# Products of attention weights and values of two units in one PSUM bank of their own, behind each other

## The chip, the cores and the metric

The kernel runs on one core of one Trainium2 chip. The metric is the device time in microseconds (us) of one execution. The engines go by the names of the profile: PE is TensorE's matrix multiply, PEld its weight load, DVE is VectorE, ACT is ScalarE, POOL is GpSimd, SP is the engine that issues nearly all DMAs. Each engine runs its own instructions in the order in which they were issued to it; a wait at the head of an engine's queue holds up all that stands behind it.

## The reference

One decoder layer on 16 sequences of 128 tokens with width 256, all in float32. Three parts follow each other, each with a residual and a layer norm:

```python
# 1: causal attention, 16 heads of 16, only the 32 largest scores of a row are kept
scores = q @ k.T / sqrt(16)            # causal mask: -inf
vals, idx = top_k(scores, 32)
attn = softmax(scores kept at idx, -inf elsewhere)
x = layernorm(x + (attn @ v) @ Wo.T + bo)
# 2: 8 experts of 256 -> 512 -> 256, each token weighs every expert by its gate
o = einsum('eid,bsed->bsei', proj_out, relu(einsum('edi,bsi->bsed', proj_in, x)))
x = layernorm(x + sum_e o[..., e, :] * gate[..., e])   # gate: sums of ctx where itok == e
# 3: Hadamard transform, 4-bit rounding per token, ternary weights
x = layernorm(x + quantized(x @ H) @ ternary(weight).T)
```

## The kernel before

**Tiles and units.** The 16 sequences are cut into nine tiles t = 0 to 8 of 1, 1, 2, 2, 2, 2, 2, 2, 2 sequences (`SIZES`, L35). The attention of a tile is cut into units (t, c, b): c is one of two halves of the heads (8 heads, `HC`), b the sequence within the tile, and b runs fastest (L752). Tiles 0 and 1 have two units each (0, 1 and 2, 3); each later tile has four: units 4 to 7 are tile 2, units 20 to 23 tile 6, units 28 to 31 tile 8. The first two units of such a tile are its first half of heads (c = 0), the other two its second (c = 1).

**One unit.** `attn_scores` (L337) multiplies queries and keys into two PSUM banks, ACT copies them to `sc` (L346), POOL adds the causal mask (L352). `attn_weights` finds the 32 largest on DVE by four rounds of MAX8 (L381) and MATCH_REPLACE8 (L396), with a small scaling (L383) after the first; ACT takes exponentials (L372, L389). `attn_finish` sums them (L408), puts weights in place of the marks (L412, DVE) and divides by the sums (L416, POOL); the result is `wk`. `attn_turn` transposes `wk` on PE into two PSUM tiles, `pta` (L427, four transposes) and `ptb` (L428, one), and ACT copies them to `pT` (L437, five copies), of which there are two buffers that the units use in turn. `attn_apply` (L439) multiplies `pT` with the values `vm`: eight calls of a 32-column matmul (L445), each stored as two records in the trace, into the second quarter of the bank of `ptb`, and ACT copies the product with the bias to `oT` (L448, 128x128).

**The end of a tile.** `attn_end` multiplies `oT` by the output weights (`py`, L457), DVE adds the residual (L460) and begins a layer norm, for which ACT gives the inverse root (`rstd_a`, L230 and L232) and DVE does the rest (L239, L240, L259). PE transposes the result (L472), and the tile joins the queue of the experts.

**The experts** (`experts`, L507) are the bulk: up products (L554) into `ph`, ACT's relu (L558), down products (L521) into `po`, ACT's scaling by the gate into `part` (L529), and POOL's sum into `acc` (L532). Between them run the gates of a tile (L500 on DVE, pairs of them for two sequences), and, for the tile before, `ffn`: layer norm, Hadamard steps on POOL (L638), the rounding (L641 to L651, DVE), and the last product (L663, L618).

**What sets the order.** Nothing is planned by costs of an engine: the instructions are issued in the order of the Python program. A generator runs the attention in 9 steps a unit (`STEPS`, L789); a dictionary `plan` holds what else is done in a step (`at`, L797); and the loop at L898 puts expert work behind each step, so much that it keeps pace with the steps. The turn of a unit is 3 steps after its end (1 step for the last unit of a tile), its products are two steps behind its turn (L832):

Of the kernel before, what the change touches and what calls it, by code (L numbers as in the profile page):

```python
# [13 lines left out]
AF = mybir.ActivationFunctionType  # L14
# [3 lines left out]
P = 128  # L18
# [11 lines left out]
def decoder_kernel(ctx: ExitStack, tc: tile.TileContext, i: dict, out: bass.AP):  # L30
    nc = tc.nc
    NB, S, D = 16, 128, 256
    NH, DH, TOPK = 16, 16, 32
    E, DFF = 8, 512
    SIZES = (1, 1, 2, 2, 2, 2, 2, 2, 2)  # L35
    FIRST = [sum(SIZES[:t]) for t in range(len(SIZES))]
# [6 lines left out]
    HC = NH // DC  # L43
# [17 lines left out]
    def psum(name, dtype=F32):  # L61
        return ps.tile([P, 512], dtype, tag="ps", name=name)
# [60 lines left out]
    bv = const.tile([P, DC], F32, name="bv")  # L123
# [43 lines left out]
    def buffers(shape, n, name):  # L167
        return [const.tile(shape, F32, name=f"{name}{k}") for k in range(n)]
# [4 lines left out]
    pTs = buffers([P, HC, S], 2, "pT")  # L173

    vms = buffers([P, NH // 2, 3 * DH], 6, "vm")
# [176 lines left out]
            nc.gpsimd.tensor_tensor(d, d, m, ALU.add)  # L352
        return lambda m: sc[:, keys(m)], ins

    weights, mids = {}, {}

    def attn_weights(n, sc):

# [62 lines left out]
    def attn_turn(n):  # L421

        p = weights.pop(n)
        big = psum(f"pta{n}")
        mid = mids[n] = psum(f"ptb{n}")
        for k, at in enumerate((256, 384, 0, 128)):
            nc.tensor.transpose(big[:, ts(k, P)], p[:, at : at + P], ident)  # L427
        nc.tensor.transpose(mid[:, :P], p[:, 512 : 512 + P], ident)  # L428
        pT = pTs[n % len(pTs)]
        for rows, src, heads, q in (  # L430
            (96, big[0:96, 0:256], slice(0, 8), 64),
            (32, big[96:128, 0:256], slice(0, 8), 0),
            (128, big[:, 256:512], slice(0, 8), 96),
            (64, mid[0:64, :P], slice(0, 4), 32),
            (64, mid[64:128, :P], slice(4, 8), 32),
        ):
            nc.scalar.copy(pT[0:rows, heads, q : q + 32], src.rearrange("p (h q) -> p h q", q=32))  # L437

    def attn_apply(n, vm, oT, c, b):  # L439
        pT = pTs[n % len(pTs)]  # L440
        av = mids.pop(n)[:, P : P + S]
        for k in range(2):
            for g in range(4):
                h = 2 * g + k
                nc.tensor.matmul(  # L445
                    av[ts(g, 32)], vm[:, c * HC // 2 + g, k * DH : (k + 2) * DH], pT[:, h], start=k == 0, stop=k == 1
                )
        nc.scalar.activation(oT[:, c, ts(b, S)], av, AF.Identity, bias=bv[:, c : c + 1])  # L448

    def attn_end(t, oT, x):  # L450

# [301 lines left out]
    inputs, qk, outs, scores = {0: loaded, 1: next_loaded, 2: third_loaded}, {}, {}, {}  # L753
# [48 lines left out]

    def products(u):
        t, c, b = units[u]
        attn_apply(u, vms[(FIRST[t] + b) % len(vms)], outs[t], c, b)

    ending = {}

# [14 lines left out]
    for u, (t, c, b) in enumerate(units):  # L823
        s, quick = STEPS * (u + 1), u < FIRST_UNITS
        if (c, b) == (0, 0):
            at(s - STEPS, open_tile, t)
        if u in lag:
            at(s + lag[u], attn_finish, u)
        late = lag.get(u, 0)
        turn = s + (0 if quick else late + 2 if u in lag else 1)  # L830
        at(turn, attn_turn, u)
        at(turn + 2, products, u)  # L832
        if u == LAST[t]:
            for k in (2, 3, 4, 4) if quick else (4, 6, 8, 9):
                at(s + k, end, t)
            for k in (-3, -1, *range(5, 5 + E)) if quick else (-5, -3, *range(9, 9 + E)):
                at(s + k, next_of_gates, t)
            at(s - 1, next_gates, t + 2)
# [59 lines left out]
    for step, _ in enumerate(attention()):  # L898
        for fn in plan.get(step, ()):
            fn()  # L900
        while done < pace(step):
            c = next(work)
# [48 lines left out]
```

**PSUM.** All of `pta`, `ptb`, the scores, `py`, and a few more come from one pool of four banks (`ps`, L54, through `psum`, L61), taken in a ring in the order of issue: a new tile waits until the readers of the tile four before it are done. Expert products have two pools of two banks each.

## Time and profile before

| | |
|---|---|
| Median of three runs | 643.68 us (642.24 to 644.35) |
| The profiled execution | 643.58 us |
| Its span, first to last instruction | 641.9 us |
| Mean granted TensorE clock | 0.983 |
| L445, products | 512 records, 0.273 us each (median), overlapping |
| L448, copy of a product, 128x128 | 32, 0.350 us each (median) |
| L428, transposes into `ptb` | 32, 0.272 us each (median) |
| L383, scaling of the maxima, DVE | 32, 0.172 us (median), 0.822 at most |
| L532, sums of the experts, POOL | 64, some 1.27 us for two sequences |

A row of the timeline gives the start in us from the beginning of the span, the duration, the engine, the line, the operation, what is written and read (partitions x elements), and the count of instructions merged into the row; in square brackets stands the idle time of the engine ahead of it and what ended it. A row with a count runs from the first start to the last end. A row of the waits gives the waiting instruction, what it waited for, the total in us, how often, and the longest. In the page's chain each share is that of an engine in the chain of work that ended last.

### The profile page before, as it was taken

What the parts mean: (1) busy time and instruction counts of PE and PEld (TensorE: products, weight loads), DVE (VectorE), ACT (ScalarE), POOL (GpSimd) and SP (SyncE); (2) the same over time, 40 slices, a digit from 0 to 9 for tenths busy, and PEclk for the clock granted to TensorE, in tenths of its full rate; (3) what the DMA queues carried; (4) which work ended last, traced back from release to release, by engine and by line L of the source; (5) the groups of instructions that cost most, each with busy time, mean ns of one, the idle gap of its engine ahead of it and who ended that gap; (6) DMA issues with size and microseconds to landing.
All of it is one profiled execution on the core that took longest, in us unless ns stands there. A gap on an engine that the chain in (4) does not pass through costs nothing.

```text
span 641.9 us, 12499 instructions
## 1 busy us (share of the span) xinstructions
PE 608.2 (95%) x3534; PEld 523.6 (82%) x3534; DVE 500.9 (78%) x3128; ACT 346.4 (54%) x1030; POOL 306.4 (48%) x578
## 2 busy tenths in 40 slices
PE   6669999989999999999999999999999999999993
PEld 5459888878888888888888888888888888888882
DVE  6989799789956996789957898569978997332246
ACT  4746666755566565556555555656555655432122
POOL 6204554433663367424773457434673458324323
PEclk9869999999999999999999999999999999999997
DMA  6175800010001000010000000000000000000000
GB/s 205 16 221 170 279 5 9 18 41 2 10 17 38 22 2 17 9 42 2 9 18 18 25 2 10 1 14 13 2 2 0 18 2 10 1 17 0 1 2 33
DMA packets 38134, 21.20 MB, mean 33 GB/s; under 512 B 19120, under 2 KB 36016, under 8 KB 38064
## 3 DMA queue, kind: packets, MB, share of 16 engines
q1 hardware_dynamic: 37504, 20.26, 10.8%
q8 instruction: 28, 0.46, 0.3%
q14 instruction: 42, 0.34, 0.2%
q10 hardware_dynamic: 560, 0.13, 0.1%
HBM read 16.32 MB, written 2.10 MB: 29 GB/s over the span
## 4 chain that ended last, share of the span: by engine, by line
PE 77%; DVE 11%; ACT 5%; POOL 2%; issue 2%; DMA 1%; SPq 1%; ACTq 0%; DVEq 0%; POOLq 0%
PE ph L554 30%; PE po L521 28%; PE ps L337 4%; PE pqk L272 3%; DVE wk L396 3%; PE ptb L445 2%; PE py L457 2%; PE pta L427 2%; DVE m L381 2%; POOL wk L416 2%; PE pv L316 1%; DVE junk L500 1%; ACT ex L372 1%; DVE wk L412 1%; ACT pT L437 1%
## 5 line engine op out<-in xcount | busy, mean ns | idle before, releaser
L554 PE MATMUL ph<-x1T,w_in 128*128 128x256 f32 (+1 forms) x1152 | 240.7, 358 | 0.7 <-ACT hT L558 0.6
L521 PE MATMUL po<-w_out,hT 128*128 128x256 f32 x1024 | 238.4, 381 | 0.0
L554 PEld LDWEIGHTS ph<-x1T,w_in 128*128 128x128 f32 x1152 | 198.6, 190 | 26.7 <-issue 3.4
L521 PEld LDWEIGHTS po<-w_out,hT 128*128 128x128 f32 x1024 | 189.6, 190 | 24.5 <-issue 1.4
L558 ACT ACTIVATE hT<-ph 128x512 f32<-128x512 f32 (+1 forms) x144 | 78.9, 549 | 134.0 <-PE ph L554 133.6
L396 DVE MATCH_REPLACE8 wk<-m,wk 128x64 f32<-128x64 f32 (+2 forms) x576 | 132.1, 240 | 0.0
L529 ACT ACTIVATE part<-po,gate 128x256 f32<-128x256 f32 x112 | 52.9, 472 | 93.4 <-PE po L521 92.8
L381 DVE MAX8 m<-wk 128x8 f32<-128x64 f32 (+2 forms) x576 | 100.5, 242 | 0.0
L416 POOL TENSOR_TENSOR wk<-wk,rz 128x128 f32<-128x128 f32 (+2 forms) x92 | 47.4, 540 | 93.6 <-DVE wk L412 93.6
L532 POOL TENSOR_TENSOR acc<-acc,part 128x512 f32<-128x512 f32 (+1 forms) x56 | 64.4, 1149 | 46.7 <-ACT part L529 46.0
L372 ACT ACTIVATE ex<-sc,nb 128x32 f32<-128x32 f32 (+1 forms) x248 | 74.2, 350 | 0.0
L638 POOL TENSOR_TENSOR xh<-xh 128x256 f32<-128x256 f32 x98 | 67.8, 713 | 1.2
L352 POOL TENSOR_TENSOR sc<-sc,cmask 128x64 f32<-128x64 f32 (+1 forms) x93 | 32.1, 372 | 56.6 <-ACT sc L346 56.6
L337 PEld LDWEIGHTS ps<-kT,qblk 128*128 128x128 f32 x256 | 41.7, 195 | 5.4 <-POOL qblk L303 1.4
L396 DVE MATCH_VALUE_LOAD wk<-m,wk 128x8 f32 x576 | 44.9, 78 | 0.0
L337 PE MATMUL ps<-kT,qblk 128*128 128x256 f32 (+3 forms) x256 | 43.5, 314 | 1.3 <-ACT qblk L301 1.0
L396 DVE MATCH_REPLACE8 wk<-m,sc 128x64 f32<-128x64 f32 (+1 forms) x186 | 42.7, 241 | 0.0
L500 DVE SCALAR_TENSOR_TENSOR junk<-wt 128x128 f32<-128x128 f32 x128 | 42.4, 362 | 0.0
L437 ACT COPY pT<-pta 96x256 f32<-96x256 f32 (+2 forms) x96 | 35.2, 366 | 6.3 <-PE pta L427 5.5
L381 DVE MAX8 m<-sc 128x8 f32<-128x32 f32 (+1 forms) x248 | 38.3, 226 | 0.0
L641 DVE TENSOR_REDUCE qs<-xh 128x2 f32<-128x512 f32 x7 | 4.8, 685 | 36.0 <-POOL xh L638 36.0
L427 PE MATMUL pta<-ident,wk 128*128 128x128 f32 x128 | 20.2, 281 | 11.4 <-POOL wk L363 7.7
(178 smaller groups left out, 671.5 us busy)
## 6 DMA issues: line engine op xcount, KB each, us to landing
w_in<-in_w_in SPq DMA_DIRECT2D x8, 512.0 KB, 6.1
w_out<-in_w_out SPq DMA_DIRECT2D x8, 512.0 KB, 7.2
xT<-in_xT SPq DMA_DIRECT2D x7, 256.0 KB, 3.8
x<-in_x SPq DMA_DIRECT2D x7, 256.0 KB, 2.8
qblk<-qT SPq DMA_DIRECT2D x112, 16.0 KB, 1.9
out_y<-y SPq DMA_DIRECT2D x7, 256.0 KB, 2.1
ctx<-in_ctx SPq DMA_DIRECT2D x7, 128.0 KB, 2.1
tok<-in_itok SPq DMA_DIRECT2D x7, 128.0 KB, 2.1
```

The lines of the kernel that those rows point to most:

```text
L337: ins = nc.tensor.matmul(view(parts[PLACE[0, j] // 512], at, [[step, 2], [1, 32 * (j + 1)]]), qblk[:, b, j].rearrange("p h q -> p (h q)"), ...
L372: nc.scalar.activation(ex[:, keys(m)], sc(m), AF.Exp, bias=nb[:, m : m + 1], scale=SCALE, accum_out=z[:, m : m + 1] if m < 2 else None,)
L381: nc.vector.max(m8[:, m, ts(r, 8)], left(m))
L396: nc.vector.match_replace(wk[:, keys(m)], m8[:, m, ts(r, 8)], left(m), TAKEN)
L416: eng.tensor_tensor(view(wk, at, [[step, 2], [1, size]]), view(src, at, [[step, 2], [1, size]]), rz[:, 2 * j : 2 * j + 2].unsqueeze(2).to_ ...
L500: nc.vector.scalar_tensor_tensor(junk, wt[:, 1, b], float(e), wt[:, 0, b], ALU.is_equal, ALU.mult, accum_out=gate[:, b, e : e + 1],)
L521: nc.tensor.matmul(po, hT[:, f, ts(b, S)], w_out[:, e, f], start=f == 0, stop=f == FC - 1)
L529: nc.scalar.activation(part[:, b], po, AF.Copy, scale=gates[t][:, b, e : e + 1])
L532: sums.append(lambda: nc.gpsimd.tensor_tensor(acc[:, :n], (acc if e else x1)[:, :n], part[:, :n], ALU.add))
L554: nc.tensor.matmul(ph[:, f, : n * S], w_in[:, e, c, ts(2 * k + f, P)], x1T[:, c, : n * S], start=c == 0, stop=c == DC - 1,)
L558: ins = nc.scalar.activation(hT[:, ts(k, 2), : n * S], ph[:, :, : n * S], AF.Relu)
L638: nc.gpsimd.tensor_tensor(pairs(xh, c, half), pairs(from_, 0, half), pairs(from_, 1, half), op)
```

## The change

The products of a unit are no longer made two steps after its own turn. `products` does nothing for the first of two sequences; for the last one, `attn_apply` makes the products of all units of that tile and half, one behind the other, in a new PSUM tile `pav` of the ring (128 columns for each unit), and one copy takes the whole to `oT`. The tile `ptb` holds only its transpose now. In tiles 0 and 1, with one sequence, the step of the products stays, and only the bank is new.

```diff
-    weights, mids = {}, {}
+    weights = {}
...
         big = psum(f"pta{n}")
-        mid = mids[n] = psum(f"ptb{n}")
+        mid = psum(f"ptb{n}")
...
-    def attn_apply(n, vm, oT, c, b):
-        pT = pTs[n % len(pTs)]
-        av = mids.pop(n)[:, P : P + S]
-        for k in range(2):
-            for g in range(4):
-                h = 2 * g + k
-                nc.tensor.matmul(
-                    av[ts(g, 32)], vm[:, c * HC // 2 + g, k * DH : (k + 2) * DH], pT[:, h], start=k == 0, stop=k == 1
-                )
-        nc.scalar.activation(oT[:, c, ts(b, S)], av, AF.Identity, bias=bv[:, c : c + 1])
+    def attn_apply(us, t, c):
+
+        size = len(us) * S
+        av = psum(f"pav{us[0]}")[:, :size]
+        for b, n in enumerate(us):
+            vm, pT = vms[(FIRST[t] + b) % len(vms)], pTs[n % len(pTs)]
+            for k in range(2):
+                for g in range(4):
+                    h = 2 * g + k
+                    nc.tensor.matmul(
+                        av[ts(g, 32), ts(b, S)], vm[:, c * HC // 2 + g, k * DH : (k + 2) * DH], pT[:, h],
+                        start=k == 0, stop=k == 1,
+                    )
+        nc.scalar.activation(outs[t][:, c, :size], av, AF.Identity, bias=bv[:, c : c + 1])
...
     def products(u):
         t, c, b = units[u]
-        attn_apply(u, vms[(FIRST[t] + b) % len(vms)], outs[t], c, b)
+        if b == SIZES[t] - 1:
+            attn_apply(range(u - b, u + 1), t, c)
```

## The prediction

> **What bounds the kernel now.** First the page's busy rows and the chain that ended last. PE is busy 95% and holds 77% of the chain, but DVE holds 11% and the multiply of the weights on POOL (L416) 2%. So TensorE sets the pace, with places where the attention's own chain is last.
>
> ```profile
> PE 608.2 (95%) x3534; PEld 523.6 (82%) x3534; DVE 500.9 (78%) x3128; ACT 346.4 (54%) x1030; POOL 306.4 (48%) x578
> PE 77%; DVE 11%; ACT 5%; POOL 2%; issue 2%; DMA 1%; SPq 1%; ACTq 0%; DVEq 0%; POOLq 0%
> ```
>
> Second, who waited for whom: what PE waits for, after the start, is mostly `wk` at the turn (L427), once the copies of `pT`.
>
> ```profile
> PE pta L427 <- POOL wk L363: 7.7, 4, 5.0
> PE ptb L445 <- ACT pT L437: 4.4, 3, 2.1
> PE pta L427 <- POOL wk L416: 3.7, 5, 1.3
> ```
>
> Third, the timeline of one tile, t=6 (units 20 to 23), PE and DVE and POOL:
>
> ```profile
> 355.35 0.27 DVE L239 TENSOR_SCALAR var_a<-var_a,rstd_a 128x1 f32<-128x1 f32 x1 [3.25 <-ACT rstd_a L232]
> 364.03 0.66 PE L427 MATMUL pta<-ident,wk 128*128 128x128 f32 x4 [0.49 <-POOL wk L416]
> ...
> 367.23 1.03 PE L554 MATMUL ph<-x1T,w_in 128*128 128x256 f32 x4
> 368.18 0.65 PE L445 MATMUL ptb<-pT,vm 128*32 128x128 f32 x16
> 368.76 0.48 PE L554 MATMUL ph<-x1T,w_in 128*128 128x256 f32 x1
> ...
> 379.93 0.34 POOL L416 TENSOR_TENSOR wk<-ex,rz 128x64 f32<-128x64 f32 x1
> 380.42 0.60 PE L427 MATMUL pta<-ident,wk 128*128 128x128 f32 x4
> ```
>
> DVE waits at 355.35 for an ACT queue that PE paces, and then has no idle time until the Hadamard wait at 406.50: the weights of units 20 and 21 are pure DVE and POOL work from 355.35 on. Unit 20's turn waits (364.03). Unit 21's weights are ready at 379.93+0.34 = 380.27, and PE turns them at 380.42: **a slack of 0.15**, of which about 0.05 is the semaphore. The same 0.15 or 0.16 stands at the second unit of t=3 to 8; in t=3, 6, 7, 8 the first unit waits. From unit 21's turn to the next tile's `rstd_a` PE has no gap; the turns of units 22 and 23 have 1.2 and 2.8 of slack.
>
> **The price of a block of products.** L554 starts each 0.216 us (16 in 3.62 less the last one's 0.38, over 15 steps). The last before the block starts at 367.23+3x0.216 = 367.88, the next after it at 368.76: 0.88, where 0.216 would do. So a block costs 0.67: 0.31 into the 32-column shape, 0.37 for its four rounds of four column groups, 0.20 out. Four more rounds at the 0.11 between rounds (0.65 less a last one of 0.27 is 0.38 for three steps, the first of 0.13) are 0.44.
>
> **The change part by part.**
> 1. The first unit's block goes: PE is 0.67 earlier from there on. In unit 4 also the 0.88 wait for `pT` goes.
> 2. The second unit's block gets 8 products more: +0.44. A pair thus frees 0.23; 14 pairs (t=2 to 8, two halves each) are 3.2 us of PE. t=0 and 1 have one unit and stay.
>    Here I weigh a rule of the Trainium skill, TensorEngine Tiling (Array Packing), Key Properties: a change of tiling mode drains TensorE. By the rule alone a pair saves one whole entry and exit, and 3.2 us would come off the end (640.4). The row (0.31 in, 0.20 out) agrees with the price, but the rule says nothing of what comes next, and the rows of L427 do: the freed time lies ahead of a turn with 0.15 of slack.
> 3. Copies: 14 of L448 go (0.35 each), 14 become 256 wide. The nearest row is L288, 128x256 with a bias from PSUM, 0.47: +0.12. ACT gains 3.2 us at 54% busy; behind the wider copy at the tile's end py (L457) has the down block of 1.95 as cover. Value 0; if that cover went, 7x0.12 = 0.8.
> 4. Banks: 18 new tiles in the ring of four. The bank that `pav` takes was, in the first half, the next unit's first score bank (freed by L346, 0.59 long, over a us before the block), in the second half the unit's own `pta`, whose copies the products need anyway; `ptb` is free sooner, at its copies. Value 0, at worst one L346, 0.6, where ACT is late (t=2), and below nothing 0.2.
> 5. `pT` of the first unit lives until the pair. Its buffer is written again at the turn of unit+2: 22's copies come some 16 us after the pair of 20 and 21. Value 0. Products of the pair still wait for the second unit's copies, with at least 0.5 of slack (t=2, unit 5) and now 0.44 of ready products ahead.
> No DMA moves.
>
> **Where the time goes, tile by tile.** Take unit 21's turn: PE arrives 0.67 sooner, but its weights are ready only 0.10 sooner than used. If DVE is not moved, the turn comes 0.10 earlier, the pair costs +0.44, the second half -0.67+0.44: a tile costs 0.44-0.67+0.44-0.10 = **+0.11**, not -0.46. So 0.21 less what the turn gains (at most 0.67).
>
> DVE is moved, though, since POOL's sums of the experts (L532) are paced by PE through ACT's `part`, and DVE and POOL get in each other's way. The first sum of the tile, and DVE's work near it (t=5, then t=6; last a pair at 568, where DVE lost):
>
> ```profile
> 299.32 0.28 DVE L500 SCALAR_TENSOR_TENSOR junk<-wt 128x128 f32<-128x128 f32 x1
> 300.29 1.26 POOL L532 TENSOR_TENSOR acc<-x,part 128x512 f32<-128x512 f32 x1 [1.09 <-ACT part L529]
> 300.81 0.78 DVE L383 TENSOR_SCALAR nb<-m 128x8 f32<-128x8 f32 x1
> ...
> 374.00 0.28 DVE L500 SCALAR_TENSOR_TENSOR junk<-wt 128x128 f32<-128x128 f32 x1
> 374.20 0.29 DVE L500 SCALAR_TENSOR_TENSOR junk<-wt 128x128 f32<-128x128 f32 x1
> 374.80 1.27 POOL L532 TENSOR_TENSOR acc<-x,part 128x512 f32<-128x512 f32 x1 [0.88 <-ACT part L529]
> 375.69 0.40 DVE L383 TENSOR_SCALAR nb<-m 128x8 f32<-128x8 f32 x1
> ...
> 567.93 1.27 POOL L532 TENSOR_TENSOR acc<-acc,part 128x512 f32<-128x512 f32 x1 [1.26 <-ACT part L529]
> 567.95 1.40 DVE L500 SCALAR_TENSOR_TENSOR junk<-wt 128x128 f32<-128x128 f32 x1
> ```
>
> L383 takes 0.17 alone; here it ends with L532 (0.78, 0.40). At 567.95 L500, 0.28 alone, takes 1.40: it comes just behind L532 and waits it out. Move L532 by 0.67:
> - t=5: 299.62, just behind L500 (ends 299.60); it ends at 300.89, and L383 is done some 0.58 sooner. The turn gains the full 0.67: -0.46. t=3 likewise (L532 from 152.57 to 151.90, behind L228 of 151.69; L383 0.82 there): -0.46.
> - t=6: 374.13, between the starts of the two L500. L532 then runs to 375.40, and the second L500 ends 0.14 after it, as at 568 (569.35 against 569.20): 375.54 instead of 374.49, so 1.05 lost. L383 regains 0.23. The weights come 0.82 later, the turn, with its slack of 0.10, 0.72 later, and the tile costs 0.21+0.72 = +0.93. t=7 (L500 at 448.51 and 448.72, L532 to 448.64) and t=8 (517.71, 517.91, to 517.83) stand the same: +0.93 each.
> - t=4: 225.77 against L228 at 225.82, a toss-up: +0.83 or -0.28; I take +0.3.
> - t=2: the turn of unit 5 waits already (1.1), so the 0.67 and the 0.88 of unit 4 are lost, and the turn of unit 7 waits too (0.46), for sums (L408) that wait 3.2 for ACT's queue behind PE. The pair of 4 and 5 makes that queue 0.44 later, the dropped L448 0.25 sooner; then the pair of 6 and 7 puts 0.44 on the way to py, on which DVE waits (0.89): +0.6, between 0 and 1.2.
>
> Here the second rule: SBUF — State Buffer, section SBUF: two separate sides, says that the port pair that DVE shares with GpSimd is a lock, kept for a whole instruction by whoever starts first. By it the first L500 of t=6 keeps L532 out and L532 then follows, which is my +0.93. One row speaks otherwise: at 366.30 two L500 ran one behind the other (0.28 the second) and the L532 issued at the same time took 1.41. If DVE passes on to its second L500 in this way, L532 starts 0.36 later, t=6 to 8 cost +0.21-0.25 each, and 2.9 us fall away. L532 would come 0.07 ahead of the second L500; at 567.95, 0.02 ahead, POOL won. I take the loss.
>
> Sum: 0.6-0.46+0.3-0.46+3x0.93 = **+2.8** on the profiled 643.58 (span 641.9): 646.4. It stands 0.1 below the runs' median of 643.68; predicted 646.4.
>
> **Rivals.**
> A. The above: 646.4, own range 644.8 to 648. For it: four rows of L532 standing beside a pair of L500 or L228. Against it: it hangs on 0.07 us of phase. 0.53.
> B. Lead and cost cancel: the turns gain 0.1 to 0.25, DVE keeps its second L500, t=4 goes well: 0.6-0.46-0.28-0.46-0.1 = -0.7, 643.0; 641.9 to 644.6. 0.26.
> C. Faster: the L532 that come sooner free DVE in every tile, as in t=3 and 5. The place is L383, the price 0.67 a tile; it decides where the second unit's weights come 0.57 sooner. Six tiles at -0.46 and t=2 at +0.6: 641.4; with t=2 at its share 640.4. Against it: L383 loses only 0.23 in t=6 to 8, so there is little to free. 0.12.
> D. A new wait in the ring of banks, or L532 also on the pair of L500 in t=5 (+1.7 instead of -0.46): 648 to 650. 0.08.
> E. That the change does not do what it says, the two units' products not standing together on PE: their 16 calls are in one function and PE runs them in the order of issue; 0.01 at most, and with the time of before.
>
> **How the numbers follow.** Within 0.3% (about what a measurement of this kernel can tell from no change) is 641.75 to 645.61. A lies above it in three of four: 0.40 slower, 0.13 same. B: 0.23 same, 0.03 faster. C: 0.10 faster, 0.02 same. D: 0.08 slower. E: 0.01 same. Faster 0.13, same 0.39, slower 0.48. The range 641.8 to 648.0 leaves out most of C and of D.
>
> **What would show it.** Right: L445 in blocks of 32 of about 0.82 from first to last start; 18 of L448, 14 at 0.47; PE's idle before L427 grown by 3 to 5 us while PE's busy sum falls by some 3; the second L500 ahead of L383 at 1.3 to 1.4 in t=6 to 8, and L383 at 0.17 there. Wrong: L427 of the second units without idle time (C), or those L500 at 0.29 with L532 at 1.6 (B). A PE wait before L445 for ACT's L346 would be D.

## The result and the profile after

The changed kernel takes 646.84 us (median of 6, 645.94 to 648.58), the kernel before beside it 643.56 (median of 6, 642.24 to 644.61). The ratio is 1.005, with a 95% interval from 1.0036 to 1.0065: slower by 0.5%. The profiled execution of the changed kernel took 645.94, its span is 644.2. Three executions among those of the experiments below, of 723, 2058 and 3587 us, lie far outside all others and are left out of the medians and ratios.

The lines have new numbers: products L448, their copy L452, py L461, down products L525, `part` L533, the sums on POOL L536, up products L558, the gates L504, the last product's use of `pf` L622. First the page, its busy row and the chain by engine:

```profile
PE 603.9 (94%) x3534; PEld 523.9 (81%) x3534; DVE 503.3 (78%) x3128; ACT 345.4 (54%) x1016; POOL 306.3 (48%) x578
PE 62%; DVE 25%; ACT 6%; POOL 3%; issue 2%; DMA 1%; SPq 1%; ACTq 0%; DVEq 0%; POOLq 0%
```

PE works 4.3 us less than before (608.2), 3.0 of them from unit 4 on (536.5 against 539.5), and the kernel is longer all the same: PE's share of the chain that ended last has gone from 77% to 62%, DVE's from 11% to 25%. What PE waited for (total in us, times, longest):

```profile
PE pta L427 <- POOL wk L416: 9.0, 9, 1.4
PE pta L427 <- POOL wk L363: 8.1, 4, 5.2
PE pav L448 <- ACT pT L437: 3.0, 2, 1.8
PE ph L558 <- ACT hT L562: 2.5, 2, 2.3
```

The waits of the turn for `wk` were 7.7 and 3.7, in sum 11.4; they are 17.1. The timeline of tile 6, where before the second unit's turn had no wait, PE alone:

```profile
363.59 0.66 PE L427 MATMUL pta<-ident,wk 128*128 128x128 f32 x4 [0.50 <-POOL wk L416]
364.19 5.35 PE L558 MATMUL ph<-x1T,w_in 128*128 128x256 f32 x24
...
380.75 0.66 PE L427 MATMUL pta<-ident,wk 128*128 128x128 f32 x4 [1.37 <-POOL wk L416]
...
384.90 1.08 PE L448 MATMUL pav<-pT,vm 128*32 128x128 f32 x32
```

From unit 20's turn to unit 21's it was 16.39 us; it is 17.16, though the block of products in between is gone (L558 runs on, 24 in a row) and PE now waits 1.37 at the end. Why the weights come late is seen on POOL and DVE, in tile 6 and then in tile 4:

```profile
373.59 1.41 POOL L536 TENSOR_TENSOR acc<-x,part 128x512 f32<-128x512 f32 x1 [0.36 <-ACT part L533]
373.59 0.28 DVE L504 SCALAR_TENSOR_TENSOR junk<-wt 128x128 f32<-128x128 f32 x1
373.80 1.34 DVE L504 SCALAR_TENSOR_TENSOR junk<-wt 128x128 f32<-128x128 f32 x1
376.34 0.17 DVE L383 TENSOR_SCALAR nb<-m 128x8 f32<-128x8 f32 x1
...
224.49 1.27 POOL L536 TENSOR_TENSOR acc<-x,part 128x512 f32<-128x512 f32 x1 [6.73 <-ACT part L533]
224.56 1.22 DVE L228 TENSOR_SCALAR var_e<-mv_e 128x2 f32<-128x2 f32 x1
```

In the kernel before, the same two in tile 4:

```profile
226.44 1.27 POOL L532 TENSOR_TENSOR acc<-x,part 128x512 f32<-128x512 f32 x1 [7.41 <-ACT part L529]
225.82 0.17 DVE L228 TENSOR_SCALAR var_e<-mv_e 128x2 f32<-128x2 f32 x1
```

In tile 6 POOL's sum came between the two gates, and the second took 1.34 instead of 0.29; L383 is back at 0.17. In tile 4 the sum came 0.07 ahead of L228, which took 1.22 instead of 0.17.

**Tile by tile.** To lay the traces side by side I take the start of the first L427 of each tile's first unit, and the end of the span for the last, each less the same in the kernel before, set to zero at unit 4; the difference from one to the next is what a tile adds. The names at the head are those of the experiments below.

| tile | changed | own bank | moved alone | first half | second half | late sum | spread, before | spread, changed | later scores |
|---|---|---|---|---|---|---|---|---|---|
| 2 | +0.63 | +0.01 | +0.63 | +0.44 | +0.20 | +1.40 | -2.12 | -1.87 | -1.88 |
| 3 | 0.00 | 0.00 | 0.00 | -0.26 | +0.26 | -0.02 | 0.00 | -0.09 | -0.74 |
| 4 | +1.36 | 0.00 | +1.34 | +1.07 | +0.27 | +0.25 | 0.00 | +0.03 | +0.04 |
| 5 | -0.51 | +0.01 | -0.54 | -0.21 | -0.33 | -0.55 | -0.65 | -1.22 | -1.22 |
| 6 | +0.93 | 0.00 | +0.94 | +1.25 | -0.33 | -0.14 | -0.71 | -1.28 | -1.28 |
| 7 | +0.93 | -0.01 | +0.92 | +1.25 | -0.33 | -0.16 | -0.57 | -1.15 | -1.14 |
| 8 | +0.93 | 0.00 | +0.92 | +1.23 | -0.33 | -0.11 | +0.61 | +0.30 | +0.30 |
| sum | +4.27 | +0.01 | +4.22 | +4.79 | -0.59 | +0.67 | -3.45 | -5.28 | -5.92 |

The sum of +4.27 is more than the +2.35 between the spans (641.86 and 644.21), since the changed kernel's profiled execution reached unit 4 1.92 us sooner. That is no work of the change: between 20 and 30 us PE's granted clock was 0.83 in the profiled execution before and 1.00 in that after. The row of that stretch (us, busy time and instructions of each engine, then the granted clock) before:

```profile
20.00:30.00 10.00, 6.39 (x40) 4.87 (x39) 9.93 (x69) 6.11 (x22) 2.18 (x7) 0.83 0.10 16
```

and after:

```profile
20.00:30.00 10.00, 5.12 (x39) 3.98 (x39) 9.93 (x72) 7.79 (x26) 2.19 (x7) 1.00 0.11 17
```

The start differs so from execution to execution, whatever the kernel. Of the eleven traces (the kernel before, the changed one and nine experiments), five with 0.83 to 0.87 in this stretch begin unit 4's turn at 85.93 to 86.99 us, five with 1.00 at 83.93 to 84.43, among these the control below, which makes the products as the kernel before does. The eleventh (late sum) has 1.00 here, but 0.66 between 60 and 65 us, and begins it at 87.28. The medians, 3.3 us apart, are taken over executions of both kinds.

### The profile page after: what moved, and what is told of

Its sections match the earlier page's. It is cut to its first block, busy times and chain, and to the rows that moved or that the text cites. A ratio compares the mean times of both kernels' runs of the same rounds, so it can differ in the third digit from the quotient of the medians.

```text
span 644.2 us, 12490 instructions
## 1 busy us (share of the span) xinstructions
PE 603.9 (94%) x3534; PEld 523.9 (81%) x3534; DVE 503.3 (78%) x3128; ACT 345.4 (54%) x1016; POOL 306.3 (48%) x578
## 4 chain that ended last, share of the span: by engine, by line
PE 62%; DVE 25%; ACT 6%; POOL 3%; issue 2%; DMA 1%; SPq 1%; ACTq 0%; DVEq 0%; POOLq 0%
PE po L525 23%; PE ph L558 23%; DVE wk L396 7%; DVE m L381 5%; DVE junk L504 4%; PE ps L337 3%; PE pqk L272 3%; PE pav L448 2%; POOL wk L416 2%; PE py L461 2%; PE pta L427 2%; ACT ex L372 1%; DVE wk L412 1%; PE pv L316 1%; ACT pT L437 1%
## 5 line engine op out<-in xcount | busy, mean ns | idle before, releaser
L558 PE MATMUL ph<-x1T,w_in 128*128 128x256 f32 (+1 forms) x1152 | 237.7, 357 | 2.9 <-ACT hT L562 2.5
L525 PE MATMUL po<-w_out,hT 128*128 128x256 f32 x1024 | 238.4, 381 | 0.0
L558 PEld LDWEIGHTS ph<-x1T,w_in 128*128 128x128 f32 x1152 | 199.5, 190 | 27.5 <-ACT hT L562 3.4
L525 PEld LDWEIGHTS po<-w_out,hT 128*128 128x128 f32 x1024 | 189.6, 190 | 24.5 <-issue 1.4
L533 ACT ACTIVATE part<-po,gate 128x256 f32<-128x256 f32 x112 | 53.0, 473 | 92.7 <-PE po L525 90.5
L536 POOL TENSOR_TENSOR acc<-acc,part 128x512 f32<-128x512 f32 (+1 forms) x56 | 64.4, 1150 | 53.5 <-ACT part L533 53.0
L504 DVE SCALAR_TENSOR_TENSOR junk<-wt 128x128 f32<-128x128 f32 x128 | 45.5, 386 | 0.0
L427 PE MATMUL pta<-ident,wk 128*128 128x128 f32 x128 | 20.5, 284 | 17.0 <-POOL wk L416 9.0
```

Source lines behind the costliest of these rows:

```text
L504: nc.vector.scalar_tensor_tensor(junk, wt[:, 1, b], float(e), wt[:, 0, b], ALU.is_equal, ALU.mult, accum_out=gate[:, b, e : e + 1],)
L525: nc.tensor.matmul(po, hT[:, f, ts(b, S)], w_out[:, e, f], start=f == 0, stop=f == FC - 1)
L533: nc.scalar.activation(part[:, b], po, AF.Copy, scale=gates[t][:, b, e : e + 1])
L536: sums.append(lambda: nc.gpsimd.tensor_tensor(acc[:, :n], (acc if e else x1)[:, :n], part[:, :n], ALU.add))
L558: nc.tensor.matmul(ph[:, f, : n * S], w_in[:, e, c, ts(2 * k + f, P)], x1T[:, c, : n * S], start=c == 0, stop=c == DC - 1,)
```

## The experiments

My theory: without the first unit's block, PE runs ahead of its former times (its lead). Ahead of the second unit's turn nearly all of that lead is spent waiting, since the weights came just in time before; and until then it moves POOL's sum onto DVE's gates (tiles 6 to 8) or onto L228 (tile 4). Rivals: the new bank in the ring, the common bank or the wider copy, and the end of the tile behind a pair. The first four kernels take the change apart.

**Own bank.** Each unit's products stay in place. In this and the next three kernels `attn_apply` also writes a single unit to its own columns of `oT`; these lines are left out here.

```diff
-        if b == SIZES[t] - 1:
-            attn_apply(range(u - b, u + 1), t, c)
+        attn_apply([u], t, c)
```

> The bank alone: each unit's products stay at their own place and have a copy of their own, but in a new bank of the ring. If the cost is where PE stands ahead of the second unit's turn, nothing has moved: 643.6 as before, within 0.4. If the new tiles in the ring of four make PE wait, most of the 3.3 us is here: 645 to 647, and PE has waits ahead of L448 for ACT's L346.

Measured: 643.73 against 643.53, ratio 1.000 (0.9983 to 1.0017). In the table no tile moves by more than 0.01. The ring of banks with 32 more tiles costs nothing while the products stand where they stood.

**Moved alone.** Both units' products together, each with its own bank and copy.

```diff
         if b == SIZES[t] - 1:
-            attn_apply(range(u - b, u + 1), t, c)
+            for n in range(u - b, u + 1):
+                attn_apply([n], t, c)
```

> The move alone: the products of both units stand one behind the other, but each unit has its own bank and its own copy of 128 columns. If the cost comes from the place of the products, it is all here: 646.8 as the changed kernel, within 0.5. If it comes from the common bank or from the wider copy, this kernel is at 643.6 to 645.

Measured: 646.12, ratio 1.0047 (1.0028 to 1.0066), and each tile of the changed kernel to 0.03. The common bank and the joint copy are worth nothing either way; it is the place of the products.

**First half and second half.** Pairs only where c = 0, or only where c = 1.

```diff
-        if b == SIZES[t] - 1:
+        if c:
+            attn_apply([u], t, c)
+        elif b == SIZES[t] - 1:
             attn_apply(range(u - b, u + 1), t, c)
```

> Pairs in the first half of heads (c = 0) alone. If L532 meets DVE's pair of L500 (tiles 6 to 8) or L228 (tile 4) because PE runs ahead of the second unit's turn, the cost is here and undiluted: +1.25 in tiles 6, 7 and 8, +1.1 in tile 4, -0.25 in tiles 3 and 5, +0.3 in tile 2, in sum +4.6: 648.2. If the cost is what stands behind a pair at a tile's end (a later copy, a later py), this kernel is at 643 to 644.

> Pairs in the second half (c = 1) alone. By the meeting of L532 and DVE in the first half, nothing is lost here: -0.33 in tiles 5 to 8, about +0.1 in tiles 3 and 4 where PE, being ahead, waits some 0.45 for a bank that DVE's L618 still reads, +0.2 in tile 2: 642.7. By a cost at the tile's end: 645 to 647.

Measured: first half 649.05, ratio 1.0084 (1.0062 to 1.0106); second half 642.68, ratio 0.9987 (0.9976 to 0.9999). The tiles are those expected: +1.25, +1.25, +1.23 in 6 to 8, +1.07 in 4, -0.26 and -0.21 in 3 and 5; and -0.33 in tiles 5 to 8 for the second half. What the turn waits for `wk`, first half alone:

```profile
PE pta L427 <- POOL wk L416: 8.9, 9, 1.4
```

and second half alone, as in the kernel before:

```profile
PE pta L427 <- POOL wk L416: 3.7, 5, 1.3
```

So the net cost is in the first halves, and the pairs of the second halves gain 0.6 in sum. A cost at the tile's end is ruled out as the main one: with it the second half alone would have been slow; in tile 2 it costs 0.20. In tiles 3 and 4 the second half loses 0.26 and 0.27, where 0.1 was expected; that is the bank of `pf` (below).

**Late sum.** The changed kernel, with one small POOL instruction ahead of the first sum of four tiles' experts.

```diff
+    spare = const.tile([P, 1], F32, name="spare")
...
-                sums.append(lambda: nc.gpsimd.tensor_tensor(
-                    acc[:, :n], (acc if e else x1)[:, :n], part[:, :n], ALU.add
-                ))
+                def add():
+                    if e == 0 and t in (3, 5, 6, 7):
+                        nc.gpsimd.tensor_scalar(spare, part[:, n - 1, D - 1 :], 0.0, None, ALU.mult)
+                    nc.gpsimd.tensor_tensor(acc[:, :n], (acc if e else x1)[:, :n], part[:, :n], ALU.add)
+
+                sums.append(add)
```

> The changed kernel, with one more POOL instruction of one column (some 0.3 us) ahead of the first sum (L532) of the experts of tiles 3, 5, 6 and 7, which run in the windows of tiles 4, 6, 7 and 8. L532 then comes behind the start of the second L500 and behind L228. If their meeting is the cause: the second L500 back to 0.29, the second unit's turn 0.8 to 1.0 earlier in four tiles, 643.0 in all. If the place of L532 is not the cause: 646.8.

Measured: 643.81, ratio to the kernel before 1.0005 (0.999 to 1.002). Tile 6 in the timeline (all lines one higher and more here: the sum is L540, the gates L505, the turn L428):

```profile
376.47 0.28 DVE L505 SCALAR_TENSOR_TENSOR junk<-wt 128x128 f32<-128x128 f32 x1
376.68 0.28 DVE L505 SCALAR_TENSOR_TENSOR junk<-wt 128x128 f32<-128x128 f32 x1
376.47 0.36 POOL L539 TENSOR_SCALAR spare<-part 128x1 f32<-128x1 f32 x1 [0.36 <-ACT part L534]
376.79 1.30 POOL L540 TENSOR_TENSOR acc<-x,part 128x512 f32<-128x512 f32 x1
382.56 0.65 PE L428 MATMUL pta<-ident,wk 128*128 128x128 f32 x4 [0.31 <-POOL wk L417]
```

The small instruction now starts level with the first gate, and the sum 0.11 behind the start of the second; both gates take their usual 0.28, and PE's wait at the turn is 0.31 instead of 1.37. Tiles 6 to 8 go from +0.93 to -0.14, -0.16 and -0.11, tile 4 from +1.36 to +0.25: 4.3 us. The meeting thus costs some 1.1 us in each of the four. Tile 2, which the edit does not touch, has +1.40 here instead of +0.63. In this execution the granted clock was 0.74 between 95 and 100 us, within tile 2; in the ten other traces it was 1.00 there. That fits the difference, but was not tested apart.

**The control**: the same instruction in the kernel before.

> The control for the late sum: the same POOL instruction in the kernel before. There L532 already runs into L383 (0.40 in tiles 6 to 8, 0.56 in tile 4); 0.3 later it should hold L383 up 0.3 longer, of which 0.10 is slack: +0.2 in each of four tiles, 644.4. If the instruction were a help in itself, this kernel would be 3 us faster, as the late sum made the changed kernel.

Measured: 644.63, ratio 1.001 (0.9992 to 1.0027): no gain. By the same account as in the table it adds 0.15 in tile 4 and 0.16, 0.14 and 0.16 in tiles 6 to 8, with L383 there at 0.59 instead of 0.40. The instruction helps only where the pair has put the sum on the gates.

**Spread of the gates.** If the lead is lost because the second unit's weights are late, it must pay where they are early. Three pairs of L500 stay ahead of those weights instead of eight, none ahead of the first unit's.

```diff
-            for k in (-3, -1, *range(5, 5 + E)) if quick else (-5, -3, *range(9, 9 + E)):
+            for k in (-3, -1, *range(5, 5 + E)) if quick else (-5, -3, 11, 14, 17, 20, 22, 24, 26, 28):
```

> The kernel before, with the pairs of L500 spread: steps 11, 14, 17, 20, 22, 24, 26, 28 after a tile's end instead of 9 to 16, so that two pairs leave DVE's way to the first unit's weights and five its way to the second's. The waits of the first unit's turn (1.4, 0.65, 0.65, 0.5 in tiles 3, 6, 7, 8) and some of tile 2 should go: 639 to 641. It is the base for the next.

> The changed kernel with the same spread of L500. If a pair frees PE time that is lost only because the second unit's weights are late, it shows now that they are not: 0.33 for each of 14 pairs, less some 0.9 for the wait for L618's bank in tiles 3 and 4: 3 us under the kernel before with the same spread. If pairs are dear in themselves, it is 3 us over it.

Measured: 640.62 without pairs, ratio to the kernel before 0.9944 (0.9925 to 0.9963); 636.93 with them, 0.9899 (0.988 to 0.9918). Tile 6 with pairs and spread, the turns of units 20 and 21 on PE:

```profile
361.54 0.60 PE L427 MATMUL pta<-ident,wk 128*128 128x128 f32 x4
377.20 0.60 PE L427 MATMUL pta<-ident,wk 128*128 128x128 f32 x4
```

No wait at either, 15.66 us apart instead of 16.39: the lead is now kept. The spread does two things at once, since the sum, now at 371.57, meets no gate either; what the meeting alone costs is told by the late sum. The pairs, slower by 3.3 us before, are faster by 3.7 in the medians, and by 1.8 from unit 4 on in the traces (5.28 less 3.45), where 3 were expected. By tiles: -0.57 each in 5 to 7, -0.31 in 8, nothing in 3 and 4, +0.25 in 2. A second set of runs beside the next experiment:

> The changed kernel with the spread of L500 again, beside the one with the later scores on the same chip: 636.9, within 0.6.

Measured: 639.04, ratio 0.9922 (0.9899 to 0.9946), over the 636.9 within 0.6 that was expected; no trace of it is used. Against the 640.62 without pairs, from another chip, that is 1.6: the sign holds, and the size from the medians is loose.

**Later scores.** What keeps tiles 3 and 4 from gaining? On top of the spread, the scores of units 13 and 17 are issued one step later.

```diff
-        at(STEPS * u + (5 if u == FIRST_UNITS else 1), score, u + 1)
+        at(STEPS * u + (5 if u == FIRST_UNITS else 2 if u in (12, 16) else 1), score, u + 1)
```

> The changed kernel with the spread of L500, and the scores of units 13 and 17 issued one step later. If PE's waits of 0.33 (a step of 0.66 instead of 0.22) ahead of those scores are the bank that DVE's L622 still reads, they go, and tiles 3 and 4 are 0.45 shorter each: 0.9 under the kernel with the spread alone, 636.0. If the wait only moves to the next user of the bank, no difference.

Measured: 637.62, ratio 0.991 (0.9888 to 0.9932), as against 0.9899 and 0.9922 for the spread alone: the times do not tell. The traces do: tile 3 is 0.65 shorter, and the wait is gone there; tile 4 has not moved by more than 0.01. In tile 4 no expert work is issued between the two steps, so that the edit changed nothing in PE's order. Half of the expectation holds, and half was not tested.

## Why the prediction was right

It forecast 646.4, slower, by the case called A; measured were 646.84, and the two steps of A, the wait at the turn and the sum on the gates, are what the runs show. Point by point:

- **The slack of the second unit's turn** held: the lead is lost in tiles 4, 6, 7, 8, and the first-half kernel shows the cost undiluted.
- **The gates of tiles 6 to 8**: +0.93 each, measured +0.93 each. That it fits to the hundredth is luck in part: the working has +1.16 for the first half and -0.23 for the second, and the two kernels with one half measured about +1.25 and -0.33. The second L500 was put at about 1.3 to 1.4 and is 1.34. Of the two outcomes weighed there, DVE did not pass on to its second gate. The sum came even sooner than computed, level with the first gate instead of 0.13 behind, since the lead is larger than I had it. It waited for that one alone (1.41 instead of 1.27).
- **Tile 5**: -0.46, measured -0.51. **Tile 2**: +0.6, measured +0.63, in the steps of the working: +0.44 by the first half alone, +0.20 (0.44 less 0.25) by the second.
- **Tile 4**, the toss-up: the sum came ahead of L228. The branch of +0.83 is the one that came, and 0.53 more. The first half is as computed (+1.07; in the working 1.06, that is 0.83 without the -0.23 of the second half); the second adds 0.27 instead of -0.23, which is the next point.
- **Tile 3** failed: -0.46, measured 0.00. The step at fault is the value 0 for the banks, where I looked only at what the new tile `pav` waits for, and the sentence that PE has no gap from the second turn on, which I had read in tile 6 and put on all tiles. In tiles 3 and 4 `pf` stands four places ahead of a unit's second score bank, so that these scores wait for DVE's L618. Before:

```profile
193.10 1.33 PE L337 MATMUL ps<-kT,qblk 128*128 128x256 f32 x8
...
192.84 0.88 DVE L618 SCALAR_TENSOR_TENSOR y<-pf,qs,wfs 128x256 f32<-128x256 f32 x2
```

After:

```profile
190.79 0.92 PE L337 MATMUL ps<-kT,qblk 128*128 128x256 f32 x4
192.05 0.66 PE L337 MATMUL ps<-kT,qblk 128*128 128x128 f32 x4 [0.34 <-DVE y L622]
...
191.13 0.86 DVE L622 SCALAR_TENSOR_TENSOR y<-pf,qs,wfs 128x256 f32<-128x256 f32 x2
```

  Before, DVE was done at 193.72, just ahead of the second bank's first score at 193.86. With PE ahead by the block that is gone, the scores wait for DVE's end at 191.99: 0.6 of the lead is lost, in tile 3 and again in tile 4. With the gates spread, moving the scores gave it back in tile 3.
- **The price of a block** was too small: 0.67 taken, 0.77 measured, as the second L554 behind a block, too, starts late (0.32 behind the first instead of 0.22). The eight products more cost 0.44, as taken; a pair thus frees 0.33, which is what the second halves of tiles 5 to 8 gain. PE's busy sum fell by 3.0 from unit 4 on, as forecast; the other 1.3 of its fall lie ahead of unit 4, where the clocks differed.
- **The copy** became 0.458 in the median for 256 columns (0.47 taken from L288) and is on no path: with its own copies the kernel is the same.

The tiles cost 4.27 in sum, where 2.8 was computed; the missing 1.5 is in tiles 3 (0.46) and 4 (1.06). That the forecast came within 0.5 us of the measured median is thus luck in part: it was counted from one profiled execution, and executions differ by some 2 us at the start, of which no step spoke. Whether that alone makes the medians' 3.3 less than the traces' 4.27 is not shown.

## What to carry to other kernels

An engine that is busy 95% of the time gains from less work only up to its next wait: look at the slack of the next instruction that needs another engine's result, tile by tile, and at what else the engine paces. Here work taken off TensorE brought a sum on GpSimd forward by 0.8 us into VectorE's path; with VectorE's gates moved out of that path (and nothing else) the same change saves 1.8 us from unit 4 on instead of costing 4.3. Read the ring of banks for all its users, not only for the new tile.

## What had not been expected of the hardware

- A GpSimd sum of 128x512 that started level with the first of two VectorE instructions got in between them: the sum took 1.41 instead of 1.27, the first VectorE instruction its usual 0.28, the second 1.34. So it was in three tiles (sums at 373.59, 449.03 and 519.16, second gates of 1.34 each). In the kernel before, the second of such a pair had started level with a sum and kept it waiting:

```profile
366.30 0.28 DVE L500 SCALAR_TENSOR_TENSOR junk<-wt 128x128 f32<-128x128 f32 x1
366.30 1.41 POOL L532 TENSOR_TENSOR acc<-acc,part 128x512 f32<-128x512 f32 x1
```

  A tenth or two of a microsecond decide 1.05 us: in the late sum's trace the sum starts 0.11 behind the second gate, which takes its 0.28.
- Behind a block of 32-column products not only the first 128-column matmul is late (0.20) but also the second, by 0.10.
- With the granted clock at 0.83 to 0.87 instead of 1.00 between 20 and 30 us, unit 4 began some 2 us later, in kernels of both kinds. Timings of one kernel show it too: the changed kernel's three executions with a mean clock of 0.985 took 645.94 to 646.54, the three with 0.982 took 647.13 to 648.58.
